# A four-layer image network on one core: the first batch's statistics from 384 rows, and a batch's last weights by two wide products

## The chip, the core and the metric

The kernel runs on one core of one Trainium2 chip. The metric is device time in microseconds (us) of one execution; smaller is better. The engines of the core work side by side, each through its own list of instructions in order: TensorE (PE, with its weight loads PEld), VectorE (DVE), ScalarE (ACT), GpSimd (POOL), and SyncE (SP), which here only issues DMAs. A DMA is issued by an engine's queue and then runs on 16 DMA engines that all queues share.

## The reference

The input `x` is `(4, 48, 256, 256)`, float32. Four layers are applied, each as `x = x + layer(group_norm(x))` with 16 groups of 3 channels:

- Layer 0: a 1x1 convolution to q, k, v, a 3x3 convolution by channel, attention between the channels of each image (48x48, from the l2-normalised q and k), and a 1x1 projection.
- Layer 1: a gated network over tokens (48 to 16, GELU twice, layer norm, two small convolutions, gate, 8 to 48).
- Layers 2 and 3: four recurrent scans over rows and columns (down, up, right, left), in each step a convolution over the width or height with 48x48x5 weights.

The change lies in layer 0. What it needs:

```python
def _gn(v, G=16, eps=1e-5):
    g = v.reshape(B_, G, C_ // G, H_, W_)
    m = jnp.mean(g, axis=(2, 3, 4), keepdims=True)
    s = jnp.var(g, axis=(2, 3, 4), keepdims=True)
    return ((g - m) / jnp.sqrt(s + eps)).reshape(v.shape)

qkv = conv1x1(gn(x), qkv_w); qkv = conv3x3_by_channel(qkv, dw_w)
q, k, v = split(qkv)
attn = softmax(l2n(q) @ l2n(k).T * temperature)
x = x + conv1x1(attn @ v, proj_w)
```

So each image needs the mean and variance of each group of channels before anything else of layer 0 can be done with it.

## The kernel before, in words

`program` calls `layers01` (layers 0 and 1) and then `scans` (layers 2 and 3). A scheduler orders the instructions of each engine and puts in the waits; tiles come from pools, and a tile that takes over the memory of another waits for the last reader of that memory.

**First batch's statistics (L182 to L200).** `input_stats(0, i)` loads one of 16 pieces of batch 0: a tile `sx` of 96 rows (48 channels of the upper half of the image, 48 of the lower) by 2,048 elements, by two DMAs of 48 rows each on SP's queue. `sums_p` holds two such tiles, and `ahead` issues a load one piece before its use. `add` makes four `bn_stats` of 512 columns on VectorE. After the last piece one `bn_aggr` gives mean and variance by row, and `group_norm` (L80 to L107) averages them over the rows of a group by a product with a constant matrix (`mean6`), once for the means and once for the variances, and leaves a scale and a shift (`coef`).

**The other batches' statistics** use the same loads, but ScalarE sums them (`rough`, L155) while TensorE works on the batch before.

**The weights' preparation (L203 to L233)** loads `wqk`, `inside`, `pick` and others on SP's queue and multiplies them out on VectorE (`wd`, `w0`, `w1`, `wc`). The scheduler puts these between the steps of the first `group_norm`.

**The Gram sums (L526 to L569).** q and k are never made. Instead products of the image with shifted copies of itself are summed. `load_pair` loads two image rows by strip as `raw` (128 partitions, 1,728 KB, four tiles in the `patch` pool); `center` (L291) subtracts the group means; `points` (L300) makes `still` and `moving` tiles, two of each, in the same pool; `sums` (L317) multiplies them on TensorE into PSUM. There are 16 units to a batch, 64 in all. Between them stand, in small pieces (`late`), the loads and statistics of the next batch and the attention of the batch before.

**The attention's end.** `keep_project` (L481) holds the projected attention once for each of the nine taps (`pa`, 48 x 9 x 48). `taps` (L486) multiplies each by the value weights, nine products of 48 columns into one PSUM tile `pw`, and `weights` (L492) copies them and sorts them into `wy`. It runs twice for each batch: in the sums of the next batch, and for batch 3 in the convolution of batch 0.

**The convolution (L571 to L691).** After the sums the `patch` pool is closed and the pool `a_big` takes its memory: `t` (two tiles of 1.5 MB, loaded by L593), `x1n` and `x2n` (the normalised input, written by ScalarE in `norm`, L596, with edges zeroed on GpSimd) and `y`. L642 and L651 are its products with `wy`. Then comes the gated layer, in step with the convolution of the other batches, and the scans, whose products (L1151) are more than half of the time.

Of the kernel before, what the change touches and what calls it, by code (L numbers as in the profile page):

```python
# [9 lines left out]
F32 = mybir.dt.float32  # L10
AF = mybir.ActivationFunctionType
ALU = mybir.AluOpType
# [4 lines left out]
B, C, H, W = 4, 48, 256, 256  # L17
G = 16
P = 96
HW = H * W  # L20
R = 16
NB = H // R
PH, PW = 16, 32
HALO = PW + 4
NPT = 4
# [84 lines left out]
def ahead(items, load, work):  # L110

    items = list(items)
    loaded = load(items[0])
    for i, item in enumerate(items):
        now = loaded
        if i + 1 < len(items):
            loaded = load(items[i + 1])
        work(item, now)


@with_exitstack
def layers01(ctx, tc, x, xp, xe, inside, pick, xc, x1, wqk, dwqk, wv, dwv, projT, temp, k, coef, coef1, gated, spare):

# [8 lines left out]
    nc = tc.nc  # L134
    yp = ctx.enter_context(tc.tile_pool(name="a_y", bufs=1))
    small_p = ctx.enter_context(tc.tile_pool(name="a_small", bufs=2))
    p_small = ctx.enter_context(tc.tile_pool(name="a_ps", bufs=1, space=PSUM))
    sctx = ExitStack()
    wp = sctx.enter_context(tc.tile_pool(name="a_w", bufs=1))
    sums_p = sctx.enter_context(tc.tile_pool(name="a_sums", bufs=2))  # L140
    work = sctx.enter_context(tc.tile_pool(name="a_work", bufs=2))
    one = sctx.enter_context(tc.tile_pool(name="a_one", bufs=1))
    pctx = ExitStack()
    patch = pctx.enter_context(tc.tile_pool(name="a_patch", bufs=2, side="right"))
# [3 lines left out]

    n_st = M * W
    mean = [work.tile([P, 1], F32, tag="mean0", name=f"mean0_{b}", bufs=B) for b in range(B)]  # L150
    stat = [work.tile([P, 4 if b else NB * 4, 6], F32, tag=f"st0_{b > 0}", name=f"st0_{b}") for b in range(B)]
    shifted = {}
    seen = work.tile([P, n_st], F32, tag="seen", name="seen", bufs=1)

    def rough(b, i, t):  # L155

        if i == 0:
            first = work.tile([P, 2], F32, tag="first", name="first")
            nc.vector.bn_aggr(first, stat[b].rearrange("p a b -> p (a b)"))
            away = work.tile([P, 1], F32, tag="away", name="away")  # L160
            nc.vector.tensor_scalar_mul(away, first[:, 0:1], -1.0)
            sums = work.tile([P, 2, NB - 1], F32, tag="sums", name="sums")
            shifted[b] = first, away, sums
            return
        first, away, sums = shifted[b]
        for s, func in enumerate((AF.Identity, AF.Square)):
            kept = t if s else seen
            nc.scalar.activation(kept, t, func, bias=away, accum_out=sums[:, s, i - 1 : i])
        if i < NB - 1:
            return  # L170
        tot = work.tile([P, 2], F32, tag="tot", name="tot")
        nc.vector.reduce_sum(tot, sums, axis=AX.X)
        nc.vector.tensor_scalar_mul(tot, tot, 1.0 / (NB * n_st))
        mv = work.tile([P, 2], F32, tag="mv0", name="mv0")
        nc.vector.tensor_sub(mv[:, 0:1], tot[:, 0:1], away)
        d = work.tile([P, 1], F32, tag="tot2", name="tot2")
        nc.vector.tensor_mul(d, tot[:, 0:1], tot[:, 0:1])
        nc.vector.tensor_sub(d, tot[:, 1:2], d)
        nc.vector.scalar_tensor_tensor(mv[:, 1:2], first[:, 1:2], 1.0 / NB, d, ALU.mult, ALU.add)
        k.group_norm(work, p_small, mv, "mean6", coef[b], mean[b])  # L180

    def input_stats(b, i):  # L182
        t = sums_p.tile([P, n_st], F32, tag="sx", name="sx")
        for h in range(2):
            p0 = h * HW // 2 + i * n_st
            nc.sync.dma_start(t[h * C : (h + 1) * C], x[b * C : (b + 1) * C, p0 : p0 + n_st])

        def add():
            for c in range(4 if b == 0 or i == 0 else 0):
                nc.vector.bn_stats(stat[b][:, i * 4 + c, :], t[:, c * 512 : (c + 1) * 512])  # L190
            if b > 0:
                rough(b, i, t)
            elif i == NB - 1:
                mv = work.tile([P, 2], F32, tag="mv0", name="mv0")
                nc.vector.bn_aggr(mv, stat[b].rearrange("p a b -> p (a b)"))
                k.group_norm(work, p_small, mv, "mean6", coef[b], mean[b])

        return add

    ahead(range(NB), lambda i: input_stats(0, i), lambda i, add: add())  # L200


    wqk_sb = wp.tile([P, P], F32, tag="wqk", name="wqk_sb")  # L203
# [22 lines left out]
    wv_sb = wp.tile([C, 2 * 128], F32, tag="wv", name="wv_sb")  # L226
# [145 lines left out]
    def attention(b, lags, wdg, cols, ends):  # L372

        small = lambda shape, name: p_small.tile(shape, F32, tag="small", name=name)
        pj = one.tile([C, 3, 3, P], F32, tag="pj", name="pj")
        held = {}
# [108 lines left out]

        def taps(i):  # L486
            out = small([128, 3, 3, C], "pw")
            for t in range(9):
                nc.tensor.matmul(out[:, t // 3, t % 3, :], lhsT=wv_sb[:, i * 128 : i * 128 + 128], rhs=held["pa"][:, t, :], start=True, stop=True)
            held["out"] = out  # L490

        def weights(i):  # L492
# [29 lines left out]
        for i in range(2):  # L522
            pieces += [lambda i=i: taps(i), lambda i=i: weights(i)]
# [11 lines left out]
    for g in range(B * NU + 1):  # L535
        b, u = divmod(g, NU)
        if g < B * NU:
            q, part = divmod(u, 2)
# [17 lines left out]
        if g > 0:  # L556
            b, u = divmod(g - 1, NU)
# [987 lines left out]
@with_exitstack  # L1545
def program(ctx, tc, a, out, at):
    nc = tc.nc
    const = ctx.enter_context(tc.tile_pool(name="const", bufs=1))
    dram = ctx.enter_context(tc.tile_pool(name="dram", bufs=1, space=DRAM))
    k = Coefs(nc, const, at, a["cst"])  # L1550
    coefs = [
        [const.tile([P, 2], F32, tag=f"coef{layer}_{b}", name=f"coef{layer}_{b}") for b in range(B)]
        for layer in range(2)
    ]
    coef2 = const.tile([P, B, 2], F32, tag="coef2", name="coef2")
    spare = ctx.enter_context(tc.tile_pool(name="spare", bufs=2, space=PSUM))
    x1 = [dram.tile([C, HW], F32, tag=f"x1_{b}", name=f"x1_{b}") for b in range(B)]
    x2r = [dram.tile([8 * C, 8, 1024], F32, tag=f"x2r_{b}", name=f"x2r_{b}") for b in range(B)]

    def gated(ctx, tc, banks, p_small):  # L1560
        names = ("w1", "w2", "dw", "ends", "pw", "cols", "b2")
        to = [coef2[:, b] for b in range(B)]
        return gated_layer(ctx, tc, banks, p_small, x1, x2r, *(a[n] for n in names), k, coefs[1], to)

    names = ("wqk", "dwqk", "wv", "dwv", "projT", "temp")
    layers01(tc, a["x"], a["xp"], a["xe"], a["inside"], a["pick"], a["xc"], x1, *(a[n] for n in names), k, coefs[0], coefs[1], gated, spare)
    scans(tc, x2r, out, (a["c2w"], a["c3w"]), (a["c2b"], a["c3b"]), dram, k, coef2, spare)


# [8 lines left out]
def _layout(v):  # L1578

    v = {name: np.asarray(x) for name, x in v.items()}  # L1580
    a = {"x": v["x"].reshape(B * C, HW)}
    xp = np.pad(v["x"], ((0, 0), (0, 0), (1, 1), (0, 0)))
    xc = np.zeros((B, NB, 128, 12, W), v["x"].dtype)
    for n in range(NB):
        every = lambda c, h, m: xp[:, c, h + 1 : h + 2 * m : 2]
        h0, t = n * R, xc[:, n]
# [10 lines left out]
    xp = wide[:, :, h[:, None, :, None], w[None, :, None, :]].transpose(0, 2, 3, 4, 5, 1)  # L1597
# [6 lines left out]
    i = np.arange(128)  # L1604
# [3 lines left out]
    pick = np.zeros((NPT, 32, 3, 3, C))  # L1608
    for c in range(32):
        pick[:, c, :, 0, c] = by.T  # L1610
    for c in range(16):
        pick[:, c, :, 1, 32 + c] = by.T
        pick[:, 16 + c, :, 2, 32 + c] = by.T
    a["pick"] = pick.reshape(128, 9 * C).astype(v["x"].dtype)
    qkv = v["L0_conv_qkv_w"].reshape(3 * C, C)
    dw = v["L0_conv_dw_w"].reshape(3 * C, 9)
# [2 lines left out]
    c = np.arange(C)  # L1619
# [16 lines left out]
    f = np.arange(F)  # L1636
# [28 lines left out]
    f = np.arange(3 * 128)  # L1665
    line = np.repeat(np.arange(3) * NPOS, 3 * 128) - NPOS + np.tile(f // C, 3)
    for layer in (2, 3):
        ws, bs = [], []
        for way in ("down", "right", "left"):
            w = v[f"L{layer}_conv_{way}_w"]  # L1670
            t = line[:, None] - (f // C)[None] + 2
# [33 lines left out]
```

## Time and profile before

| | |
|---|---|
| median of three timed runs | 7097.66 us (7095.06 to 7098.18) |
| profiled execution, its own time | 7082.74 us |
| span of the profiled execution | 7080.7 us |
| mean granted TensorE clock | 0.97 |
| busy: PE / DVE / ACT / POOL | 94% / 51% / 26% / 29% of the span |
| start to the first Gram product | 101.4 us |
| last Gram product to the first product of the convolution | 897.1 to 906.3 us |

The page of the profile gives the busy share of each engine, the span in 40 slices (a digit is a busy share in tenths), the DMA queues, the chain of work that ended last, and the costliest groups of instructions. The trace behind it can be asked for stretches of time, for the order of instructions, and for who waited for whom. A line such as L186 is a line of the kernel before. `q1` is SP's DMA queue and `q10` ScalarE's. Each float32 product leaves two TensorE records in the trace.

### The profile page before, as it was taken

How to read it: one execution, taken by the hardware profiler on the slowest of the kernel's cores; microseconds unless marked ns; L12 is line 12 of the kernel's file. 1: busy time of each engine (PE TensorE's matmuls, PEld its weight loads, DVE VectorE, ACT ScalarE, POOL GpSimd, SP SyncE). 2: the span in 40 equal slices, each digit the busy share in tenths (PEclk: the TensorE clock that was granted, in tenths of full speed). 3: DMA queues.
4: the chain of work that ended last, by engine and by line, in shares of the span. 5: the costliest groups of instructions: out<-in, count | busy, mean ns of one | idle time of the engine just before them, and what ended most of it. 6: DMA issues, size and time to landing. Idle time of an engine off the chain costs nothing.

```text
span 7080.7 us, 133914 instructions
## 1 busy us (share of the span) xinstructions
PE 6631.8 (94%) x55886; PEld 5328.3 (75%) x55886; DVE 3644.3 (51%) x8754; ACT 1854.5 (26%) x2166; POOL 2086.7 (29%) x4211
## 2 busy tenths in 40 slices
PE   4999999999999866999998999987899999899999
PEld 3766643333333325999998999986898999899999
DVE  6777623455555554444444445754344444444444
ACT  2440012344444443443441000001354344000000
POOL 0000000233333455330002556663000000455777
PEclk9999999999999877999999999998999999999999
DMA  7752145566666676995577778988997466865775
GB/s 195 188 151 82 52 134 155 166 188 184 192 183 183 153 175 193 278 299 143 184 215 185 199 196 163 254 241 210 186 165 134 130 193 188 221 191 176 274 289 203
DMA packets 1177647, 1325.90 MB, mean 187 GB/s; under 512 B 831344, under 2 KB 1006064, under 8 KB 1124688
## 3 DMA queue, kind: packets, MB, share of 16 engines
q1 hardware_dynamic: 1164016, 1229.16, 64.3%
q10 hardware_dynamic: 12928, 87.83, 3.7%
q8 instruction: 439, 7.19, 0.4%
q14 instruction: 168, 1.38, 0.1%
q0 software_dynamic: 96, 0.33, 0.0%
HBM read 793.94 MB, written 522.19 MB: 186 GB/s over the span
## 4 chain that ended last, share of the span: by engine, by line
PE 57%; SPq 3%; DMA 3%; DVE 2%; POOL 1%; issue 1%; ACT 1%; ACTq 0%; POOLq 0%; DVEq 0%
PE ps L1151 56%; SPq L1187 2%; DMA D<-d 1%; DMA tok<-x 1%; ACT d L1226 1%; POOL s L1436 1%; DVE y L946 0%; POOL yr L951 0%; PE ph L765 0%; DVE v L864 0%; DMA near<-n 0%; DVE st L979 0%; DMA r<-R 0%; PE pout L936 0%; PE psp L897 0%
## 5 line engine op out<-in xcount | busy, mean ns | idle before, releaser
L1151 PE MATMUL ps<-d,w 128*128 128x128 f32 (+1 forms) x18360 | 2071.2, 276 | 99.7 <-DVE d L1157 61.9
L1151 PEld LDWEIGHTS ps<-d,w 128*128 128x128 f32 x18360 | 2066.4, 193 | 104.3 <-DVE d L1157 65.7
L1151 PE MATMUL ps<-r,w 128*128 128x128 f32 (+1 forms) x18360 | 2072.1, 276 | 68.9 <-POOL r L1368 35.7
L1151 PEld LDWEIGHTS ps<-r,w 128*128 128x128 f32 x18360 | 2066.3, 193 | 74.7 <-DVE r L1157 37.5
L1157 DVE SCALAR_TENSOR_TENSOR d<-ps,b,d 128x128 f32<-128x128 f32 x3054 | 979.3, 348 | 1154.0 <-PE ps L1151 1073.8
L1436 POOL TENSOR_TENSOR s<-s,r 128x128 f32<-128x128 f32 x1536 | 748.6, 522 | 332.4 <-DVE r L1157 329.9
L1157 DVE SCALAR_TENSOR_TENSOR r<-ps,b,pre 128x128 f32<-128x128 f32 x1530 | 489.9, 348 | 582.2 <-PE ps L1151 581.3
L1157 DVE SCALAR_TENSOR_TENSOR r<-ps,b,r 128x128 f32<-128x128 f32 x1530 | 489.8, 348 | 460.0 <-PE ps L1151 429.7
L324 PE MATMUL acc<-moving,raw 128*32 128x240 f32 (+1 forms) x6144 | 687.9, 382 | 11.5 <-DVE moving L307 11.5
L642 PE MATMUL py<-x1n,wy 128*96 128x512 f32 x1536 | 696.6, 602 | 1.9
L1368 POOL COPY pre<-c 128x128 f32<-128x128 f32 x1530 | 559.8, 405 | 467.5 <-DVE r L1157 464.7
L324 PE MATMUL acc<-moving,still 128*32 128x240 f32 (+1 forms) x6144 | 684.5, 382 | 6.0 <-DVE still L311 2.3
L1226 ACT ACTIVATE d<-x,spread 128x256 f32<-128x256 f32 x752 | 511.2, 827 | 544.0 <-DMA D<-d 378.1
L1307 ACT COPY u<-d 128x384 f32<-128x384 f32 x510 | 451.3, 904 | 570.7 <-DVE d L1157 509.7
L324 PEld LDWEIGHTS acc<-moving,raw 128*32 128x32 f32 x6144 | 431.5, 110 | 185.6 <-DVE moving L307 11.8
L642 PEld LDWEIGHTS py<-x1n,wy 128*96 128x96 f32 x1536 | 243.7, 164 | 413.8 <-issue 371.0
L1368 POOL COPY r<-c 128x128 f32<-128x128 f32 x6 | 2.4, 399 | 1688.9 <-DMA c<-U 1688.9
L665 DVE TENSOR_TENSOR y<-py,t 96x512 f32<-96x512 f32 x256 | 173.2, 676 | 558.8 <-PE py L651 558.8
L324 PEld LDWEIGHTS acc<-moving,still 128*32 128x32 f32 x6144 | 371.8, 110 | 35.8 <-DVE still L311 3.2
L951 POOL COPY yr<-y 96x256 f32<-96x256 f32 x512 | 316.4, 662 | 201.6 <-DVE y L946 191.1
L651 PE MATMUL py<-x2n,wy 64*96 64x512 f32 x1536 | 360.8, 601 | 0.0
L651 PEld LDWEIGHTS py<-x2n,wy 64*96 64x96 f32 x1536 | 116.5, 158 | 233.4 <-issue 229.3
(204 smaller groups left out, 4213.8 us busy)
## 6 DMA issues: line engine op xcount, KB each, us to landing
t<-in_xc SPq DMA_DIRECT2D x64, 1536.0 KB
c<-U SPq DMA_DIRECT2D x348, 256.0 KB
D<-d SPq DMA_DIRECT2D x54, 1536.0 KB
d<-D SPq DMA_DIRECT2D x54, 1536.0 KB
R<-r SPq DMA_DIRECT2D x54, 1536.0 KB
r<-R ACTq DMA_DIRECT2D x54, 1536.0 KB
U<-u SPq DMA_DIRECT2D x84, 768.0 KB
raw<-in_xp SPq DMA_DIRECT2D x36, 1728.0 KB
```

Source lines behind the costliest of these rows:

```text
L324: nc.tensor.matmul(out[32 * i : 32 * i + 32, : n * C], lhsT=still[i][:, first : first + 32], rhs=moving[:, i, lo : lo + n * C], start=u == ...
L642: nc.tensor.matmul(ps, lhsT=held["w"][0][:, dx], rhs=x1n[:, 2 * c : 2 * c + 2, dx : dx + W], start=dx == 0, stop=False)
L651: nc.tensor.matmul(held["ps"][q + 2 * s], lhsT=held["w"][1][here, dx], rhs=x2n[here, 2 * q : 2 * q + 2, dx : dx + W], start=False, stop=dx ...
L665: nc.vector.tensor_add(part, held["ps"][c], t1[:P, 2 * c : 2 * c + 2, :])
L951: nc.gpsimd.tensor_copy(yrs[c][:, :, 2 * i2 + ip, :].rearrange("p j (n a g) -> p j n a g", a=4, g=4)[:, :, :, al], y[:, i2, al].rearrange( ...
L1151: nc.tensor.matmul(ps[m][:, here], lhsT=w[:, n, :], rhs=old[:, q, there], start=first, stop=last)
L1157: nc.vector.scalar_tensor_tensor(new[:, m], ps[m], bias[:, m : m + 1], inp[:, m], ALU.add, ALU.add)
L1187: queues[q % len(queues)].dma_start(v[p0 : p0 + np_, m, 8 * n0 : 8 * n1], src[c0:c1, 8 * n0 : 8 * n1, at : at + 64])
L1226: pin(nc.scalar.activation(dst, src, AF.Identity, bias=g[:, 1:2], scale=g[:, 0:1]))
L1307: nc.scalar.copy(v[:, :, i, :, al], line)
L1368: nc.gpsimd.tensor_copy(dst[:, m].rearrange("p (J a b) -> p J a b", J=NBK, b=B), v[:, m, j, :, gl].rearrange("p J b a -> p J a b"),)
L1436: nc.gpsimd.tensor_add(v, v, line[:, m].rearrange("p (J a b) -> p J a b", J=NBK, b=B))
```

## The change

Batch 0's statistics are made from other rows: each channel is cut into eight parts, which gives 384 rows of 8,192 elements, three groups of 128. Each group is loaded in four pieces of 128 x 2,048 (1 MB), twelve loads in all, each by one DMA, with up to four under way. Every other piece takes one of the two `sx` buffers, the others a `moving` buffer of the `patch` pool, which is free at that time. `bn_stats` runs on 128 partitions, one `bn_aggr` to a group. The averages over 384 rows are three products that add up, with a new constant `rows` (loaded on ScalarE's queue), and the means are brought back to the 384 rows by three more. The other batches are left as they were. In `taps` the nine products of 48 columns become one of 432.

```diff
-    stat = [work.tile([P, 4 if b else NB * 4, 6], F32, tag=f"st0_{b > 0}", name=f"st0_{b}") for b in range(B)]
+    stat = [None] + [work.tile([P, 4, 6], F32, tag="st0", name=f"st0_{b}") for b in range(1, B)]
...
-    ahead(range(NB), lambda i: input_stats(0, i), lambda i, add: add())
+    KR, NS = 3, 4
+    rows_sb = wp.tile([128, KR * (P + 128)], F32, tag="rows", name="rows_sb")
+    nc.scalar.dma_start(rows_sb, rows)
+    to_group = lambda m: rows_sb[:, P * m : P * m + P]
+    to_row = lambda m: rows_sb[:P, KR * P + 128 * m : KR * P + 128 * m + 128]
+    stat0 = work.tile([128, KR, 4 * NS, 6], F32, tag="st0_0", name="st0_0", bufs=1)
+    x0 = x[0:C].rearrange("c (e n) -> (c e) n", e=8)
+
+    def first_stats(i):
+        m, part = divmod(i, NS)
+        if i % 2:
+            t = sums_p.tile([128, n_st], F32, tag="sx", name="sx")
+        else:
+            t = patch.tile([128, NPT * (PW // 2 + 4) * C], F32, tag="moving", name="sx")[:, :n_st]
+        nc.sync.dma_start(t, x0[128 * m : 128 * m + 128, part * n_st : part * n_st + n_st])
+
+        def add():
+            for c in range(4):
+                nc.vector.bn_stats(stat0[:, m, part * 4 + c, :], t[:, c * 512 : (c + 1) * 512])
+
+        return add
+
+    def first_norm():
+        mv = work.tile([128, KR, 2], F32, tag="mv00", name="mv00", bufs=1)
+        for m in range(KR):
+            nc.vector.bn_aggr(mv[:, m], stat0[:, m].rearrange("p a b -> p (a b)"))
+
+        def average(src, name):
+            ps = p_small.tile([P, 1], F32, tag="small", name=name)
+            for m in range(KR):
+                nc.tensor.matmul(ps, lhsT=to_group(m), rhs=src(m), start=m == 0, stop=m == KR - 1)
+            return ps
+
+        nc.vector.tensor_copy(mean[0], average(lambda m: mv[:, m, 0:1], "pg"))
+        ps = p_small.tile([128, KR], F32, tag="small", name="prows")
+        for m in range(KR):
+            nc.tensor.matmul(ps[:, m : m + 1], lhsT=to_row(m), rhs=mean[0], start=True, stop=True)
+        d = work.tile([128, KR], F32, tag="d00", name="d00", bufs=1)
+        nc.vector.tensor_sub(d, mv[:, :, 0], ps)
+        nc.vector.tensor_mul(d, d, d)
+        nc.vector.tensor_add(d, d, mv[:, :, 1])
+        s = work.tile([P, 1], F32, tag="s00", name="s00", bufs=1)
+        nc.scalar.activation(s, average(lambda m: d[:, m : m + 1], "pv"), AF.Sqrt, bias=k.eps[:P])
+        nc.vector.reciprocal(coef[0][:, 0:1], s)
+        nc.vector.scalar_tensor_tensor(coef[0][:, 1:2], mean[0], -1.0, coef[0][:, 0:1], ALU.mult, ALU.mult)
+
+    waiting = []
+    for i in range(KR * NS):
+        waiting.append(first_stats(i))
+        if len(waiting) > 3:
+            waiting.pop(0)()
+    for add in waiting:
+        add()
+    first_norm()
...
         def taps(i):
             out = small([128, 3, 3, C], "pw")
-            for t in range(9):
-                nc.tensor.matmul(out[:, t // 3, t % 3, :], lhsT=wv_sb[:, i * 128 : i * 128 + 128], rhs=held["pa"][:, t, :], start=True, stop=True)
+            nc.tensor.matmul(
+                out.rearrange("p x y c -> p (x y c)"),
+                lhsT=wv_sb[:, i * 128 : i * 128 + 128],
+                rhs=held["pa"].rearrange("p t c -> p (t c)"),
+                start=True,
+                stop=True,
+            )
```

The order of the instructions that the scheduler makes of it is the same as before but for the first stage, the two places above and single VectorE steps at changes of batch. In the addresses there is one more difference: as `moving` is now named first in the `patch` pool, its two tiles stand ahead of the four `raw` tiles, and the tiles of `a_big`, which keep their places, lie over other ones. The first `t` tile lay over the `raw` and `moving` tiles last read by unit 62 and now lies over the `raw` tile read by unit 63, the last.

More of the change, by code (lines that the diff above doesn't have):

```diff
@@ L121, in layers01 @@
 @with_exitstack
-def layers01(ctx, tc, x, xp, xe, inside, pick, xc, x1, wqk, dwqk, wv, dwv, projT, temp, k, coef, coef1, gated, spare):
+def layers01(ctx, tc, x, xp, xe, inside, pick, rows, xc, x1, wqk, dwqk, wv, dwv, projT, temp, k, coef, coef1, gated, spare):
     nc = tc.nc
@@ L188, in add @@
         def add():
[L189 to L196, printed above, removed]
-        return add
@@ L200, in layers01 @@
-    ahead(range(NB), lambda i: input_stats(0, i), lambda i, add: add())
+            if i == 0:
+                for c in range(4):
+                    nc.vector.bn_stats(stat[b][:, c, :], t[:, c * 512 : (c + 1) * 512])
+            rough(b, i, t)
+        return add
+    KR, NS = 3, 4
[3 more added lines that the diff above has]
+    to_row = lambda m: rows_sb[:P, KR * P + 128 * m : KR * P + 128 * m + 128]
@@ new lines, in layers01 @@
+    stat0 = work.tile([128, KR, 4 * NS, 6], F32, tag="st0_0", name="st0_0", bufs=1)
[8 more added lines that the diff above has]
+        def add():
+            for c in range(4):
+                nc.vector.bn_stats(stat0[:, m, part * 4 + c, :], t[:, c * 512 : (c + 1) * 512])
+        return add
@@ L1565, in program @@
     names = ("wqk", "dwqk", "wv", "dwv", "projT", "temp")
-    layers01(tc, a["x"], a["xp"], a["xe"], a["inside"], a["pick"], a["xc"], x1, *(a[n] for n in names), k, coefs[0], coefs[1], gated, spare)
+    layers01(tc, a["x"], a["xp"], a["xe"], a["inside"], a["pick"], a["rows"], a["xc"], x1, *(a[n] for n in names), k, coefs[0], coefs[1], gated, spare)
     scans(tc, x2r, out, (a["c2w"], a["c3w"]), (a["c2b"], a["c3b"]), dram, k, coef2, spare)
@@ L1613, in _layout @@
         pick[:, 16 + c, :, 2, 32 + c] = by.T
+    row = np.arange(3 * 128) // 8
+    p = np.arange(P) % C
+    at = (row[:, None] // 3 == p[None] // 3).reshape(3, 128, P) / 24.0
+    back = (np.arange(P)[:, None] == row[None]).astype(float)
+    a["rows"] = np.concatenate([*at, np.pad(back, ((0, 32), (0, 0)))], 1).astype(v["x"].dtype)
     a["pick"] = pick.reshape(128, 9 * C).astype(v["x"].dtype)
```

## The prediction

> **What bounds the kernel now.** I read the page's slices first (where TensorE is not busy), then the table of stretches for the start, then the order of time there, then the same for the two other places that the change touches. The first of the 40 slices (177 us each) has TensorE at 4 tenths; the next twelve have it at 9.
>
> ```profile
> PE   4999999999999866999998999987899999899999
> 10.00:20.00 10.00, 0.00 (x0) 0.00 (x0) 4.93 (x8) 0.00 (x0) 0.00 (x0) 1.00 0.88 184
> 70.00:78.00 8.00, 0.00 (x0) 0.00 (x0) 3.36 (x7) 0.00 (x0) 0.00 (x0) 1.00 1.03 208
> 78.00:84.00 6.00, 0.96 (x4) 0.79 (x4) 5.70 (x19) 0.31 (x1) 0.00 (x0) 1.00 1.00 407
> 84.00:96.00 12.00, 2.76 (x12) 2.63 (x12) 9.04 (x20) 2.54 (x4) 2.52 (x1) 1.00 1.02 402
> 600.00:900.00 300.00, 297.05 (x4978) 188.50 (x4969) 203.76 (x253) 10.14 (x28) 2.80 (x6) 1.00 0.21 78
> 2745.00:2753.00 8.00, 2.44 (x8) 1.85 (x8) 1.55 (x3) 6.68 (x11) 1.40 (x2) 0.50 0.99 394
> ```
>
> Columns of a stretch: its length, busy time of PE, weight loads, VectorE, ScalarE and GpSimd (instructions in brackets), granted clock, busy share of the DMA engines, GB/s. Up to 78 us no matmul runs. VectorE is busy half of the time, and the DMA engines are nearly full (0.88 to 1.03) although they move only 184 to 208 GB/s. The moment the 128-row `raw` loads follow, at 78 us, the same full share carries 402 to 407. So the batch-0 statistics are bound by loads of 48 rows that occupy the DMA engines twice as long per byte. The stretch from 600 shows the opposite: TensorE 297 of 300 us busy, so what is taken from it there is taken from the time. The last row is for later: `x<-x2r` loads, 128 rows.
>
> ```profile
> 11.94 2.46 DVE L190 BATCH_NORM_STATS2 st<-sx 96x6 f32<-96x512 f32 x4 [11.94 <-DMA sx<-in_x]
> 77.21 2.47 DVE L190 BATCH_NORM_STATS2 st<-sx 96x6 f32<-96x512 f32 x4 [1.41 <-DMA sx<-in_x]
> 79.75 1.88 DVE L195 BATCH_NORM_AGGREGATE mv<-st 96x2 f32<-96x384 f32 x1
> 90.85 3.90 DVE L298 TENSOR_TENSOR raw<-raw,means 128x3072 f32<-128x3072 f32 x3
> 101.41 1.01 PE L324 MATMUL acc<-moving,raw 128*32 128x240 f32 x2 [11.52 <-DVE moving L307]
> DVE st L190 <- DMA sx<-in_x: 40.2, 16, 11.9
> ```
>
> Start, duration, what ran, and in brackets the idle time before it and who ended it. The sixteen groups of statistics each wait for a load (40.2 us in all), the last ends at 77.21 + 2.47 = 79.68, and 11.17 us later VectorE centers the first `raw` pair. The Gram sums start at 101.41. This is a serial chain: a stage end that comes d earlier brings all that follows d earlier, as long as the `raw` loads keep up.
>
> **The change, part by part.** *The twelve loads.* They move the same 12.58 MB as the 32 before, in 1 MB pieces of 128 rows with 8 KB each at a pitch of 32 KB, four under way. Ahead or beside them go cst (0.53 MB), the new rows table (0.34), edge (0.29) and wd (0.33): 14.07 MB. The rate is the open number. The nearest row is `x<-x2r`, which also reads 128 rows at a 32 KB pitch (runs of 4 KB): 394 GB/s over 8 us with the ramp in it; the `raw` loads (pitch 121.5 KB) give 402 to 407. I take 405. [...]
>
> First bytes moved at about 1.5 us in the DMA table, with a slow first microsecond; last byte at 1.5 + 1 + 34.7 = 37.2, semaphore some 0.6 later (the `x2r` bytes ended near 2,752.8, the first reader began at 2,753.66), last group of statistics 2.5: end at 40.3. VectorE alone: first tile at about 9.5 (2.54 MB in, by the same sum), then 12 groups of about 2.55 with their gaps, and two early aggregates of 0.45 (5.50 us for 12 of that very form, 128x96, in the scans): 41.0. The two limits nearly meet, and meeting limits cost something: I take 42.0. That is 79.68 - 42.0 = **37.7 us** earlier. Ends: 39.5 (all overlaps) and 48 (358 GB/s and VectorE stalling on it): 31.7 to 40.2.
>
> *SP's queue.* A tile is loaded again only after VectorE has read it, so SP waits there with wqk, inside, pick and the four `raw` loads behind it; before, it waited in the same way (35.3 us on VectorE, 38.2 on `sx`). wqk comes just behind the last load, while the last statistics run; if it were late the first wd multiply, which stands ahead of the third aggregate on VectorE, would wait: 0 to 1 us, I take 0. `raw` 0 to 3 (1.77 MB, 4.3 us each) then land at about 44, 48, 53 and 57; center needs the first at about 54, the third some 11 us later. Covered by ten. The rows table is one more issue (0.4 us) on ScalarE's queue ahead of edge, first read at 85.74 before: nothing.
>
> *The chain of the mean.* Aggregate 1.88 becomes 0.45 for the last one (two ran early). One matmul per mean becomes three, and a hop to 384 rows (three matmuls, one subtract) is added. The scans run the same chain: their last aggregate ends at 4,887.67, the second coefficient at 4,891.80, 4.1 us, without the 1.28 us ACT table load and without wd multiplies between the steps (some 0.4). So 0.24 + 0.45 + 4.1 + 1.28 + 0.4 = 6.5 against 79.68 to 85.66 = 6.0 before: **+0.6 us** (0 to 2).
>
> *The two wide products.* A batch's weights took 18 records of 48 columns twice:
>
> ```profile
> 401.62 2.21 PE L489 MATMUL pw<-pa,wv_sb 48*128 48x48 f32 x18
> 403.75 0.44 PE L324 MATMUL acc<-moving,still 128*32 128x288 f32 x2
> 1105.88 2.21 PE L489 MATMUL pw<-pa,wv_sb 48*128 48x48 f32 x18
> 1108.01 2.82 PE L642 MATMUL py<-x1n,wy 128*96 128x512 f32 x6
> ```
>
> The next work starts 2.13 us later, every time, in the sums (batches 0 to 2) and in the convolution (batch 3), both with TensorE full. After it are 2 records of 432 columns. Twelve records of 512 columns (L642) take 5.39 us, steps of 0.43, so 432 cost 0.363 each: 0.73, and 0.8 with some start. 8 x (2.13 - 0.8) = **10.6 us** saved (0.73 gives 11.2, 1.1 gives 8.2).
>
> *What moves unasked.* Half of the early tiles take the patch pool's `moving` buffers. This names `moving` ahead of `raw` in that pool, so the addresses turn round: `t` of the first convolution block, which lay over buffers last read by sums unit 62, now lies over the `raw` tile that unit 63, the last one, reads.
>
> ```profile
> 886.83 38.15 SPq L593 DMA_DIRECT2D t<-in_xc  x3
> 897.65 2.12 ACT L599 ACTIVATE x1n<-t,g 128x2048 f32<-128x2048 f32 x1
> 904.38 1.96 PE L387 MATMUL ptap<-wdg,lag 48*48 48x288 f32 x12 [0.58 <-DVE lag L361]
> 906.27 6.25 PE L642 MATMUL py<-x1n,wy 128*96 128x512 f32 x14
> ```
>
> The load left at 886.83; now it cannot before about 897.2. Both `t` tiles ran at about 409 GB/s and were in by 896.0, so the first was in some 5.4 us after its issue, with the semaphore about 6.2: 903.4. Behind it wait x1n on ScalarE (2.12), a zeroing of 0.31 on GpSimd: 905.9 against TensorE's need at 906.27. What hides it is the lag products at 897 to 906; x2n, 1.24 later, is needed only at 912.45. If the two loads share the engines and finish together, 909.7: 3.4 late. I take **+1 us** (0 to 3.5). Behind the waiting SP stand the second `t` and the first writes, needed from 919 on. Elsewhere the orders differ in single VectorE steps (`still` after two others at one change of batch), under 1 us.
>
> **Sum**: -37.7 + 0.6 - 10.6 + 1.0 = **-46.7 us**. The profiled execution took 7082.74 (span 7080.7): 7036.0. It lies 15 below the median of the timed runs, so against 7097.66 the same difference gives **7051.0**. 0.2%, 14 us, is about what a measurement of this kernel can tell from no change.
>
> **The rivals.** *Slow loads.* The 208 GB/s at a full share belong not to 48 rows but to this tensor read by channel: then the end is at 1.5 + 1 + 14.07/0.208 + 0.6 + 2.5 = 73.2, 6.5 saved, and the sum is -15.5: 7082. For it: nothing in the trace reads `in_x` with 128 rows. Against it: `x<-x2r`, same pitch, 394. Chance 0.08.
>
> *Slower: the rows in step.* [...] Chance 0.05.
>
> *The products give nothing*: the 10.6 us turn into waits for VectorE, which has only 204 of 300 us there: -36.1, 7061. VectorE waits for TensorE (81.3 us before `still`, L309), not the reverse. Chance 0.1.
>
> *The stage does not follow the loads*: VectorE's groups grow with the rows (2.47 x 128/96 = 3.29). Twelve of 3.37 from 9.5 on, and the aggregates, end at 50.8: sum -37.9, 7060. Against it: the 128x96 aggregates cost what their columns do. Chance 0.04.
>
> **How the numbers follow.** The forecast has 0.71; its bounds give -51.4 (40.2 and 11.2 saved, nothing lost) to -34.4 (31.7 and 8.2 saved, 2 and 3.5 lost), 7046 to 7063. Idle products with their bounds reach 7072. One execution lay 15 us from the timed ones, so I widen below by 10 and above by 4: 7036 to 7076. Slow loads are half same, half faster; the rows in step slower; 0.02 is for what I don't see, half same, half slower. Faster 0.71 + 0.1 + 0.04 + 0.04 = 0.89, same 0.05, slower 0.06.
>
> **What would show it.** In the profile after: the stretches from 10 to 36 us near 400 GB/s; the last statistics ending at about 42 and the first center at about 54, first Gram matmul near 64; `raw` not waited for; two `pw` records of 432 columns with the next work 0.8 us behind; x1n of the first block some 6 us after the last sum and L642 at most 3.5 later after that sum than the 9.1 us of before. A stage end beyond 50 or a DMA rate under 300 there breaks the forecast; a first Gram matmul at 64 with a total down by less than 30 would mean that the gain is given back later.

## The result, and the profile after

The changed kernel took 7041.56 us (median of five runs, 7037.26 to 7044.79) against 7097.66 for the kernel before (five runs, 7080.98 to 7101.55): a ratio of 0.9925, 95% interval 0.9910 to 0.9939, 43 to 64 us faster. The profiled execution took 7044.79, its span is 7042.9, and its mean clock 0.969 is that of before. The first of the 40 slices is where it shows; 6 tenths of TensorE stand where 4 stood:

```profile
PE   6999999999999767999998999986898999899999
```

The table of stretches of the changed kernel at the start (length, busy time of PE, weight loads, VectorE, ScalarE and GpSimd, clock, DMA share, GB/s):

```profile
10.00:20.00 10.00, 0.00 (x0) 0.00 (x0) 8.66 (x15) 0.00 (x0) 0.00 (x0) 1.00 1.01 419
20.00:30.00 10.00, 0.48 (x2) 0.39 (x2) 9.97 (x18) 0.00 (x0) 0.00 (x0) 1.00 1.01 419
30.00:36.00 6.00, 0.48 (x2) 0.40 (x2) 5.96 (x12) 0.00 (x0) 0.00 (x0) 1.00 1.01 421
```

The DMA engines are at 1.01 and carry 419 to 421 GB/s. Before, they stood at 0.88 and 1.03 in the two stretches that the prediction shows, with 184 and 208 GB/s, and at 0.79 to 0.87 with 161 to 186 in those between. The stretch with 208 is not one of 48-row loads alone: from 75 us on it has the weights' loads and the first of `raw`, and from 70 to 75 it is 197. VectorE is now busy 9.97 of 10 us between 20 and 30: it has become a limit of this stage, level with the loads. Its order of time says the same (start, duration, what ran, idle time before and who ended it):

```profile
11.30 9.84 DVE L214 BATCH_NORM_STATS2 st<-sx 128x6 f32<-128x512 f32 x16 [11.30 <-DMA sx<-in_x]
...
39.30 2.47 DVE L214 BATCH_NORM_STATS2 st<-sx 128x6 f32<-128x512 f32 x4 [0.41 <-DMA sx<-in_x]
...
41.84 0.58 DVE L222 BATCH_NORM_AGGREGATE mv<-st 128x2 f32<-128x96 f32 x1
...
53.79 3.90 DVE L348 TENSOR_TENSOR raw<-raw,means 128x3072 f32<-128x3072 f32 x3
...
64.35 1.00 PE L374 MATMUL acc<-moving,raw 128*32 128x240 f32 x2 [11.52 <-DVE moving L357]
```

After the first tile VectorE waits for a load just once more, 0.41 us. The last statistics end at 39.30 + 2.47 = 41.77, where before they ended at 79.68: **37.9 us earlier**. The first centering (`center`, L348) begins at 53.79 (90.85 before) without a wait for `raw`, the first Gram product at 64.35 (101.41): 37.1 earlier.

The wide products, in the sums and in the convolution, with the work that follows on TensorE:

```profile
362.16 0.99 PE L538 MATMUL pw<-pa,wv_sb 48*128 48x432 f32 x2
363.08 0.44 PE L374 MATMUL acc<-moving,still 128*32 128x288 f32 x2
...
1059.59 0.99 PE L538 MATMUL pw<-pa,wv_sb 48*128 48x432 f32 x2
1060.51 1.96 PE L697 MATMUL py<-x1n,wy 128*96 128x512 f32 x4
```

The next work starts 0.92 us behind the start of `pw`, where it was 2.13. That holds at seven of the eight places; at the other it is 0.82 for 2.03. Each is 1.21 us shorter.

And the passage from the sums to the convolution, from TensorE's order of time, first the end of the sums before, then the three lines after:

```profile
896.72 0.41 PE L324 MATMUL acc<-moving,raw 128*32 128x288 f32 x1
```

```profile
849.96 0.41 PE L374 MATMUL acc<-moving,raw 128*32 128x288 f32 x1
...
857.62 1.96 PE L437 MATMUL ptap<-wdg,lag 48*48 48x288 f32 x12 [0.58 <-DVE lag L411]
859.50 1.53 PE L697 MATMUL py<-x1n,wy 128*96 128x512 f32 x3
```

From the last of the sums to the first of the convolution it is 9.54 us; before it was 896.72 to 906.27, 9.55. The first scan product starts at 2,699.9, 45.3 earlier than the 2,745.2 of before. The two spans differ by only 37.8, because the scans behind that product took 4,335.6 us in the profiled execution of before and 4,343.0 in this one. No edit touches the scans, and in the twelve profiled executions of this document they took anything from 4,332.8 to 4,344.4. The profiled execution of before was at the fast end of its kernel: 7082.74, where the timed runs have their median at 7097.66.

### The profile page after: what moved, and what is told of

Same layout as the page of the kernel before. It is cut to its first block, busy times and chain, and to the rows that moved or that the text cites. A ratio compares the mean times of both kernels' runs of the same rounds, so it can differ in the third digit from the quotient of the medians.

```text
span 7042.9 us, 133633 instructions
## 1 busy us (share of the span) xinstructions
PE 6623.6 (94%) x55772; PEld 5308.8 (75%) x55772; DVE 3630.5 (52%) x8740; ACT 1854.1 (26%) x2166; POOL 2085.2 (30%) x4211
## 4 chain that ended last, share of the span: by engine, by line
PE 56%; SPq 3%; DMA 3%; DVE 2%; POOL 1%; issue 1%; ACT 1%; ACTq 0%; POOLq 0%; DVEq 0%
PE ps L1206 55%; SPq L1242 3%; DMA D<-d 1%; ACT d L1281 1%; POOL s L1491 1%; DMA near<-n 0%; DMA tok<-x 0%; DVE y L1001 0%; DVE v L919 0%; POOL yr L1006 0%; DVE st L1034 0%; DMA r<-R 0%; DMA x2r<-yr 0%; PE ptok L873 0%; PE ph L820 0%
```

## The experiments

The timed ones (e1 to e4; thirteen runs of e2, five of each other) ran on one chip, where the kernel before took 7091.91 us (median of 17 runs, 7077.04 to 7100.76). The others (e5 to e10) are single executions, whose landmarks in the trace are read rather than their totals. On their chips the kernel before took 7100.7 (e5 to e8) and 7101.84 (e9 and e10), once each.

### The two parts, each alone, and both

`e1_statistics_alone` is the changed kernel with `taps` as before:

```diff
-            nc.tensor.matmul(out.rearrange("p x y c -> p (x y c)"), ..., rhs=held["pa"].rearrange("p t c -> p (t c)"), ...)
+            for t in range(9):
+                nc.tensor.matmul(out[:, t // 3, t % 3, :], ..., rhs=held["pa"][:, t, :], ...)
```

> The first batch's statistics as in the change, the taps as before. Theory (a serial start that comes earlier by itself): the first center at about 53.8 us and all that follows 37 us earlier, so total -37 (-31 to -42) against the kernel before. Rival (part of the 56 us measured comes from somewhere else, such as the moved addresses or the other states of the scans): the start is 37 earlier but the total differs by more than 42 or less than 31.

`e2_wide_products_alone` is the kernel before with the new `taps` (the same lines the other way round).

> Statistics as before, only the two wide products for a batch's weights. Theory (TensorE is full at all eight places): the work behind each starts 0.92 us after it instead of 2.13, 8 x 1.21 = 9.7 us less in all, the first product of the convolution 7.3 us earlier (six of the eight lie before it). Rival (the time is given back to waits for VectorE): that product no more than 2 us earlier, and the total unchanged.

`e3_change_again` is the changed kernel unaltered, in the same runs.

> The changed kernel again, beside the others: -47 to -56 against the kernel before. If the two parts are independent, e1 and e2 add up to it within their intervals; if they share a cause, it is less than their sum by more than 5 us.

| | median us | ratio to before (95%) | difference of medians |
|---|---|---|---|
| statistics alone | 7051.43 | 0.9943 (0.9929 to 0.9957) | -40.5 |
| wide products alone | 7083.46 | 0.9991 (0.9983 to 0.9999) | -8.5 |
| both | 7040.64 | 0.9929 (0.9917 to 0.9941) | -51.3 |

The parts add up: -40.5 - 8.5 = -49.0 against -51.3, well inside the intervals. So neither is seen to take from the other, and -40.5 lies in the -31 to -42 expected of the statistics. In the trace the statistics alone end their stage at 40.88 and start the Gram sums at 63.5; the wide products alone leave both within 1.1 us of where they were (78.57 and 100.3). The interval of the wide products alone ends just under 1: a gain is measured, its size (1 to 12 us) is not. The step behind each of them, 2.13 to 0.92 us, is.

In that run the first product of the convolution starts at 896.1, 10.2 us earlier than before, where 7.3 was expected and 2 or less was the rival's. One execution is a weak witness for this, so here are all whose work between the first Gram product and the first product of the convolution is the same but for `pw`. The four with the narrow products (before, e1, e5, e6) took 798.3 to 805.5 us from the one to the other, the seven with the wide ones (after, e2, e3, e7 to e10) 793.3 to 797.5. The means are 802.6 and 795.4: of the 6 x 1.21 = 7.3 us of the six places that lie there, 7.1 arrive on average.

### Depth or rows

Two things came at once in the new loads: 128 rows for 48 (or 96 by two DMAs), and four tiles under way for two. `e5_rows48_four_deep` is the kernel before, old products and old loads of 48 rows, with four tiles of 96 rows under way:

```diff
-        t = sums_p.tile([P, n_st], F32, tag="sx", name="sx")
+        if b > 0 or i % 2:
+            t = sums_p.tile([P, n_st], F32, tag="sx", name="sx")
+        else:
+            t = patch.tile([128, ...], F32, tag="moving", name="sx")[:P, :n_st]
...
-    ahead(range(NB), lambda i: input_stats(0, i), lambda i, add: add())
+    waiting = []
+    for i in range(NB):
+        waiting.append(input_stats(0, i))
+        if len(waiting) > 3:
+            waiting.pop(0)()
+    for add in waiting:
+        add()
```

> The kernel before, with its 48-row loads, but four 96-row tiles under way instead of two (half of them in the moving buffers). It tells rows from depth. Theory (48-row loads occupy the DMA engines twice as long per byte): the busy share goes from 0.87 to about 1.0 and the rate only to about 208 GB/s; last statistics end at 70 (66 to 74) instead of 79.7. Rival (two tiles under way were too few): the rate goes to about 400, VectorE becomes the bound with 16 x 2.47 us, and the end is at about 52.

The stretches of that kernel:

```profile
10.00:20.00 10.00, 0.00 (x0) 0.00 (x0) 4.94 (x8) 0.00 (x0) 0.00 (x0) 1.00 1.05 191
...
50.00:60.00 10.00, 0.00 (x0) 0.00 (x0) 6.76 (x12) 0.00 (x0) 0.00 (x0) 1.00 1.04 202
```

The DMA engines are full throughout (1.00 to 1.05 in the stretches up to 60, for 0.79 to 0.88) and carry hardly more: 187 to 202 GB/s. The stage ends at 76.21, 3.5 us before the old 79.68 and later than the 66 to 74 expected. More depth alone does not bring the 37.9 us.

`e6_rows96_one_dma` is e5 with one DMA of 96 rows to a tile. Its rows are channel by channel, each with its two halves (so 128 KB apart), an order that the group constants do not have, so the averages are over other groups of rows; the amount of work is the same.

```diff
-        for h in range(2):
+        if b == 0:
+            nc.sync.dma_start(t, x[0:C].rearrange("c (e n) -> (c e) n", e=2)[:, i * n_st : i * n_st + n_st])
+        for h in range(2 if b else 0):
```

> As e5, but each 96-row tile comes by one DMA of 96 rows (each channel in two parts, as rows c, half; its output is not the reference's, since the rows are grouped otherwise). Theory (the rate goes with the rows of a DMA): about 96/128 of 419 = 314 GB/s or more, VectorE bounds with 16 x 2.47 from about 11, end at 50.5 to 53. Rival (the 256 KB pitch between channels is what is slow): as slow as e5, end at 66 or later.

```profile
20.00:30.00 10.00, 0.00 (x0) 0.00 (x0) 7.22 (x13) 0.00 (x0) 0.00 (x0) 1.00 1.02 230
...
40.00:50.00 10.00, 0.00 (x0) 0.00 (x0) 7.26 (x13) 0.00 (x0) 0.00 (x0) 1.00 1.02 233
```

230 to 234 GB/s in the stretches from 10 to 60, the end at 65.61. Both expectations missed it: the rate does not grow in proportion to the rows (that would be 314 and an end at 50 to 53), and it is above what the pitch was to leave. Twice the rows give 15 to 20% more than the 48 at the same depth, and a third more rows on top gives another 80%.

`e7_rows128_two_deep` takes the depth away from the changed kernel:

```diff
-        if i % 2:
-            t = sums_p.tile([128, n_st], F32, tag="sx", name="sx")
-        else:
-            t = patch.tile([128, ...], F32, tag="moving", name="sx")[:, :n_st]
+        t = sums_p.tile([128, n_st], F32, tag="sx", name="sx")
...
-        if len(waiting) > 3:
+        if len(waiting) > 1:
```

> The changed kernel with only the two sx buffers, so two 128-row loads under way instead of four. Theory (rows give most of the gain, depth a smaller part): a buffer's turn is 2.5 transfer + 2.5 statistics + about 2.1 of start and completion, 7.1 for two tiles, so 12 x 3.55 + 8 = 51 for the end of the statistics (47 to 54), DMA share about 0.7. Rival A (depth gives nothing once the rows are 128): 42. Rival B (depth gives most of it): 65 or later.

```profile
10.00:20.00 10.00, 0.00 (x0) 0.00 (x0) 8.55 (x23) 0.00 (x0) 0.00 (x0) 1.00 0.87 322
20.00:30.00 10.00, 0.48 (x2) 0.40 (x2) 8.31 (x19) 0.00 (x0) 0.00 (x0) 1.00 0.88 311
30.00:40.00 10.00, 0.00 (x0) 0.00 (x0) 4.88 (x9) 0.00 (x0) 0.00 (x0) 1.00 1.01 428
```

With two under way the DMA engines have gaps (0.87 to 0.88 for 1.01), and 311 to 322 GB/s is what passes: depth is worth some 100 GB/s once the rows are 128, and next to nothing with 48. The 2.1 us of start and completion in the theory are the author's estimate; the first `t` load of the changed kernel, issued at 850.42 with the second just behind it and first read at 856.80, took 6.38 us, 2.5 more than its 1.57 MB at the 409 GB/s of the prediction. The end at 60.61 lies between what the theory (47 to 54) and rival B (65 or later) expected, so all three missed it, and it is not to be put down to depth alone. In this kernel the scheduler puts the weights' loads and the four `raw` loads between the last statistics loads on SP's queue, and from 30 us on `raw` takes its share of the 428 GB/s while VectorE waits.

### The pitch

`e8_rows128_pitch256` reads the first 2,048 columns on from 128 whole channels, so 128 rows at a pitch of 256 KB where the change has 32 KB. The statistics are those of other data.

```diff
-        nc.sync.dma_start(t, x0[128 * m : 128 * m + 128, part * n_st : part * n_st + n_st])
+        nc.sync.dma_start(t, x[0:128, i * n_st : i * n_st + n_st])
```

> The changed kernel, its twelve loads taken from 128 channels of the input at a pitch of 256 KB instead of 32 KB (so the statistics are of other data, and the output is not the reference's). Theory (rows alone): same rate, about 419 GB/s, and the same end, 41.8. Rival (the pitch between rows makes the loads slow): near 208 GB/s, end at about 73.

```profile
20.00:30.00 10.00, 0.48 (x2) 0.40 (x2) 9.96 (x18) 0.00 (x0) 0.00 (x0) 1.00 1.01 420
```

420 GB/s, the end at 41.84, 7037.08 in all. 256 KB is the pitch of the old 48-row loads. So the pitch was not what made them slow, and with 128 rows in step at 32 or 256 KB no loss shows.

### Rows of a DMA, or rows of the tile

Left open by these: does the rate belong to the rows of one DMA, or to how much of the tile's 128 rows the loads fill between them? `e9_rows64_twice` loads each piece of the changed kernel by two DMAs:

```diff
-        nc.sync.dma_start(t, x0[128 * m : 128 * m + 128, part * n_st : part * n_st + n_st])
+        for h in range(2):
+            nc.sync.dma_start(t[64 * h : 64 * h + 64], x0[128 * m + 64 * h : 128 * m + 64 * h + 64, part * n_st : part * n_st + n_st])
```

> The changed kernel with each piece of 128 rows loaded by two DMAs of 64 rows, one after the other on SP's queue, four pieces under way; nothing else. What is left open by the runs of 48 and 96 rows (187 to 234 GB/s at a full busy share) against 128 (419): does the rate belong to the rows of one DMA, or to how much of the tile's 128 rows is filled? [...] Tile filled: 400 to 420 GB/s, the end at 41.5 to 43 and the run like the changed kernel, 7036 to 7045.

```profile
20.00:30.00 10.00, 0.00 (x0) 0.00 (x0) 5.38 (x10) 0.00 (x0) 0.00 (x0) 1.00 1.02 219
...
50.00:60.00 10.00, 0.48 (x2) 0.40 (x2) 5.95 (x11) 0.00 (x0) 0.00 (x0) 1.00 1.02 219
```

219 GB/s at the same full share; VectorE, whose work is the same, is back to 5.4 to 6 us of ten, and the last group of statistics still waits 2.5 us for its load:

```profile
67.87 2.47 DVE L215 BATCH_NORM_STATS2 st<-sx 128x6 f32<-128x512 f32 x4 [2.54 <-DMA sx<-in_x]
```

The end at 70.34 lies in the 62 to 74 that were expected if the rate belongs to the rows of one DMA, and 28.6 us behind the changed kernel, with the same bytes, tiles, depth, data and order on SP's queue. So it is not how much of the tile the loads fill, but how the single DMA is cut. That each DMA now has 512 KB and not 1 MB is not it either: the `x<-x2r` loads of the kernel before have 512 KB and 128 rows, and carry 394 GB/s. Of what these runs vary, the number of rows of one DMA is left. 7066.83 in all, 23 more than the next run, on the same chip, which keeps the 128 rows.

### The moved addresses

`e10_addresses_as_before` is the changed kernel with one `raw` tile named ahead, which turns the places of `raw` and `moving` round again:

```diff
+    first_raw = patch.tile([128, 2, HALO * C], F32, tag="raw", name="raw", bufs=4)
...
-        t = patch.tile([128, 2, HALO * C], F32, tag="raw", name="raw", bufs=AHEAD + 1)
+        t = patch.tile([128, 2, HALO * C], F32, tag="raw", name="raw", bufs=AHEAD + 1) if raws else first_raw
```

> The changed kernel with one `raw` tile named in the patch pool ahead of the first statistics, so that `raw` stands ahead of `moving` again and the first `t` tile of the convolution lies over buffers that the last but one sums unit reads, as before the change. The prediction gave the moved addresses +1 us (0 to 3.5). Theory: the load of `t` leaves some 10 us earlier than in the changed kernel (about 10 us ahead of the last sums product instead of with it), x1n is written earlier, and the first product of the convolution does not move against the last sums product (9.1 to 9.3 us after it), because the products of the lag end only then: nothing gained, the run 7034 to 7045. Rival: the load costs a part of that distance, and it shrinks by 1 us or more.

TensorE's order of time in that kernel, and the order of GpSimd, whose zeroing is the last that `x1n` waits for:

```profile
852.54 0.41 PE L375 MATMUL acc<-moving,raw 128*32 128x288 f32 x1
...
860.20 1.96 PE L438 MATMUL ptap<-wdg,lag 48*48 48x288 f32 x12 [0.58 <-DVE lag L412]
862.09 0.67 PE L698 MATMUL py<-x1n,wy 128*96 128x512 f32 x1
```

```profile
855.70 0.31 POOL L657 MEMSET x1n<- 32x258 f32 x1 [2.42 <-ACT x1n L655]
```

The load of `t` leaves at 842.64, 9.9 us before the last of the sums starts (850.42 in the changed kernel, 0.5 behind it), and `x1n` is ready at 856.01, six before it is needed. Yet 852.54 to 862.09 is 9.55, as with the late load, and the run took 7043.41. The move costs nothing: the lag products, which TensorE has to do first, hide it.

### A shorter start

The stage is now followed by 12 us in which the image waits for numbers of which it needs only the mean. `e4_mean_first` makes the variance, the weights' preparation and their loads later, behind the first units' centering, and moves `cst` behind the loads of the statistics:

```diff
-        nc.sync.dma_start(self.t, cst)
+        self.load = lambda: nc.sync.dma_start(self.t, cst)
...
+    k.load()
...
-    first_norm()
+    mv_first = first_mean()
...
+            if g == 1:
+                first_var(mv_first)
+                prepare()
```

> The changed kernel, with the start further cut: batch 0's means are used for centering as soon as they are known, the variance, the scale and the weights' preparation come after the first two units of points (their loads too: the return table, wqk, pick, wv, behind raw), and cst is loaded after the twelve statistics loads. Theory (center needs only the means, the rest stands in its way on VectorE): last statistics end about 1.3 us earlier, first center at about 46 instead of 53.8, first Gram product at about 57 instead of 64.4, total 7 us (4 to 9) below the changed kernel, since VectorE has room for the 6 us of preparation beside the sums. Rival (VectorE is the bound in the first units): the first product comes earlier but the sums end at most 2 us earlier than in the changed kernel.

```profile
6.65 2.47 DVE L215 BATCH_NORM_STATS2 st<-sx 128x6 f32<-128x512 f32 x4 [6.65 <-DMA sx<-in_x]
...
45.08 3.90 DVE L359 TENSOR_TENSOR raw<-raw,means 128x3072 f32<-128x3072 f32 x3
```

```profile
55.64 1.01 PE L385 MATMUL acc<-moving,raw 128*32 128x240 f32 x2 [11.52 <-DVE moving L368]
```

The first center begins at 45.08, 8.0 us earlier than in the repeat of the changed kernel (53.10), the first Gram product at 55.6 (63.7). The sums end at 836.3, 15.3 earlier than in the repeat (851.55) and 13.7 earlier than in the first execution of the changed kernel, so the rival's 2 us at most is refuted. The median is 7034.89 (7030.92 to 7045.55), a ratio to the kernel before of 0.9924 (0.9912 to 0.9937), and 5.75 below the repeat. The landmarks are earlier beyond doubt; that the total is lower is likely and not shown, since the intervals overlap.

## Why the prediction was right

7051.0 was said (7036 to 7076, faster with 0.89); 7041.56 came. Its steps, one by one:

| step | said | measured |
|---|---|---|
| end of the statistics | 42.0 (37.7 earlier) | 41.77 (37.9 earlier) |
| from there to the first center | +0.6 | 12.02 for 11.17: +0.85 |
| a batch's `pw` twice, eight in all | 0.8 for 2.13: -10.6 | 0.92 for 2.13: -9.7 |
| moved addresses | +1.0 | 0.0 |
| sum | -46.7 | -46.75 |

*The loads.* The choice of 405 GB/s, from the trace's own 128-row loads at 394 to 407, held: 419 to 421 over 26 us. At 405 the 14.07 MB take the 34.7 us of the sum. The late end of the range, 48 us, was worked out with 358 GB/s, a rate that no run shows for these loads: 419 to 421 came in its place, and the end at 41.77. The 128-row loads were the right ones to go by, for a reason the prediction only half had. It said that loads of 48 rows hold the DMA engines twice as long per byte, and the runs of 64 rows (216 to 220 GB/s) and 96 rows (230 to 234) show that 128 is not just better but a step of its own.

*The end of the stage* came out within 0.3 us partly by luck, since two sizes missed in opposite ways. The first tile was late, 11.30 for 9.5. The prediction had counted what moves ahead and beside it, but at 405 GB/s; between 5 and 10 us the full DMA engines (share 1.04) carried 302, while `edge` and `wd`, which have 96 rows, moved beside the tile. That these two are the cause fits the rates of e6, but no run takes them away. In e4, with cst behind the tiles, the first tile is there at 6.65. VectorE then ran without the gaps that the prediction had allowed it (30.5 us for twelve groups and two aggregates; the prediction's 9.5 to 41.0 is 31.5, and 1 more for the meeting of the limits).

*The moved addresses.* The mechanism was right, the load did leave only at 850.42, behind the last unit. Its own working had it ready 0.4 us before TensorE's need and added 1 us for what might come between; zeroing ended at 859.32, 0.2 us before the 859.50 of the product, which the lag products had set. So the 0.0 is narrow: a load 0.2 us slower would have begun to show.

*The total.* Against the medians of the first runs it is -56, of the second -51.3, with intervals of some 20 us that hold the -46.7. The rest is within the spread of the kernel before, whose runs lie up to 24 us apart. Half of such a spread can come from the scans alone, which differ by up to 11.6 us between the profiled executions; why they differ was not tested (the profiled execution of before, with the shorter scans, had a granted clock of 0.976 in them, that of after 0.974). The profile's own landmarks agree with the sum: the first scan product came 45.3 us earlier.

*The rivals.* Slow loads (208 GB/s by channel): refuted, 419. The rows in step, slow because all 128 stand at one pitch: refuted, 419 to 421 at 32 KB and 415 to 420 at 256 KB; no run shows the slow rate that its chance of 0.05 was for. The products give nothing: refuted, the next work follows 1.2 us sooner each time, 7.1 of 7.3 us arrive on average at the convolution, and the run with them alone is faster, if barely by its interval. VectorE's groups grow with the rows: refuted, four of 128 x 512 take 2.47 us, as four of 96 x 512 did.

## What to carry to other kernels

Read the DMA share and the GB/s of a stretch together: full engines with half the rate (a share of 1.00 to 1.05 with 187 to 202 GB/s, and 1.01 with 419 to 421) were here a matter of how the transfer is laid out, and a row of the same trace with another layout said what there was to gain (`raw`, 402 to 407). Try 128 rows in one DMA before depth: four tiles of 48-row loads brought 187 to 202 GB/s here, two of 128-row loads 311 to 322. With 128 rows, keep enough tiles under way that the share stays at 1 (0.87 to 0.88 with two, 1.01 with four). Where a stage's limits met, the next gain lay in what was queued in front of its first tile (there at 6.65 us for 11.30) and in what the work behind it needs first (the first Gram product at 55.6 for 63.7).

## What the runs showed of the hardware

The rate against the rows of one DMA was unexpected. All these loads have rows of 8 KB. The DMA engines are full (share 1.00 to 1.05) in all but the first line, which is for the stretches from 10 to 70 us, where it is 0.79 to 0.88. The packet times are read from the records of the 8 KB packets between 10 and 60 us (10 and 36 with 128 rows), the rates from stretches in the same time:

| rows of one DMA | GB/s | median 8 KB packet, ns |
|---|---|---|
| 48, two tiles deep (before) | 161 to 186 | 577 |
| 48, four tiles deep | 187 to 202 | 672 |
| 64, four tiles deep | 216 to 220 | 609 |
| 96, four tiles deep | 230 to 234 | 573 |
| 128, four deep, pitch 32 KB | 419 to 421 | 313 |
| 128, four deep, pitch 256 KB | 415 to 420 | 313 |

From 48 to 96 rows the rate grows by a fifth; at 128 it is nearly twice that of 96, and a packet takes about half as long, nearly the same for all (309 to 320 ns for the middle 80%), while with 48 rows two deep it is anything from 377 to 892. Two DMAs of 64 rows, one for each half of the tile, carry 219 GB/s between them at a share of 1.02, with 609 ns for a packet, where one DMA of all 128 rows carries 419 at 1.01, with 313. So these runs go by the number of rows of one DMA, and not in proportion to it: 64 rows have about half the rate of 128, 96 have 230 to 234 GB/s for the 314 that three quarters of 419 would be. What makes it so is not shown: no run here separates the number of rows from another cause that goes with it, and counts between 96 and 128 were not tried.
